# Layer 0 of a four-layer graph network: the first two output tiles take their products two weight tiles behind

## The chip, the cores and the metric

The kernel runs on one core of one Trainium2 chip. A time is the device time of one execution in microseconds. Four executions of the kernel before took 2601.92 to 2609.89 us, and their median is 2607.84 us.

## The reference, cut to what matters

Sixteen graphs of 1024 nodes with 256 features go through four layers. Each layer normalizes its input, applies a relu, runs a graph layer and adds the result to its input. The first of the four is the one that is changed:

```python
h = jnp.maximum(_layernorm(x, axis=-1), 0.0)
x = x + _L0_gnn_ref(h, adj, L0_gnn_W, L0_gnn_a)

def _L0_gnn_ref(input, adj, W, a):
    h = jnp.matmul(input, W)
    f1 = jnp.einsum('bnf,f->bn', h, a1)      # a1, a2: the two halves of a
    f2 = jnp.einsum('bnf,f->bn', h, a2)
    e = jax.nn.leaky_relu(f1[:, :, None] + f2[:, None, :], negative_slope=ALPHA)
    logits = jnp.where(adj > 0, e, NEG_BIG)
    attention = jax.nn.softmax(logits, axis=1)
    h_prime = jnp.matmul(attention, h)
    return jax.nn.elu(h_prime)
```

The softmax runs over the rows (axis 1), so each column of the attention has a sum of its own. Layer 1 is the same with a softmax along the other axis, layer 2 averages over the neighbours with the plain adjacency, and layer 3 has four heads with a normalization behind it.

## The kernel before, in words

Nodes are cut into eight tiles of 128. For layer 0 of one graph the kernel first projects the eight node tiles (`project`, line 690, evicted at line 770). The logit terms of all nodes are laid out as a row in DRAM and read back to all partitions (lines 709 and 715); the first graph makes this row on TensorE instead. Then comes the loop over j = 0 to 7 that the change touches. For each j it makes one weight tile `p` of 128x1024 on VectorE: line 800 takes the larger of two products, line 802 multiplies by the mask and sums, and line 803 takes the reciprocal of the sum. Line 804 on ScalarE scales row tile j of `hs` by it. Weight tile j then serves all eight output tiles i: output tile i is the sum over j of `p[j]` (columns of i) times `hs[j]`. That is `product(ps, i, j)`, line 790.

Two of the eight output tiles (four in the first graph) are called early. They have their PSUM banks from the start of the loop, and their products are issued inside it. The other output tiles follow after the loop, one after another, each with its eight products, in the two banks of the pool `at_ps`. So output tile 2 needs the bank that output tile 0 held, which comes free when ScalarE has read it at lines 822 and 824. After each pair of output tiles the residual is written and the next layer's norm of that pair begins (lines 759, 760, 639, 671, 684).

TensorE carries out one f32 product of 128x128 with 128x256 as two passes. The products of one weight tile for two output tiles are thus four passes, shown as x4 in the rows. Layer 2 uses a rounded form of f32 with one pass for each of its adjacency products (line 922, with `hi` and `lo` parts), and f32 for the product at line 916.

Graphs overlap. The work of graph b is written as a generator that yields an estimate of time after each step, and a queue (lines 1045 to 1097) interleaves the generators by these times. Graph b+1 starts 120 units after graph b. A scheduler behind the language then sets the order in each engine's queue from its own estimates, and each engine takes its queue strictly in that order. `later(...)` is `tc.keep_in_program_order`: such an instruction keeps its place among the others that are marked. In the steady state layer 0 of a graph runs beside layer 2 of the graph before it, so the early products stand in TensorE's queue between the adjacency products of line 922.

The places that the prediction's steps touch are these: the loop and `product` of `layer0` (lines 784 to 826), the eviction of layer 2's output tiles (lines 930 and 931 on ScalarE, 932 and 760 on VectorE), the norm of the next layer (`pair` at line 639, `shifted` at line 671, `flip` at lines 684 and 685), and layer 3's projection, line 690 again, with its eviction at line 945. The loads of the adjacency are issued on POOL's queue (line 589) when an output tile of layer 2 has freed its buffer.

Of the kernel before, what the change touches and what calls it, by code (L numbers as in the profile page):

```python
# [421 lines left out]
def tile_simple_stack(  # L422
# [13 lines left out]
    NT = N // P  # L436
# [250 lines left out]
    def project(norm, w, n, width):  # L687
        ps = mm_ps.tile([P, HALF], F32, tag="mm", name="ps_proj")
        for c in range(DC):
            nc.tensor.matmul(ps[:, :width], norm.ht[:, c, n * P : (n + 1) * P], w[:, c, :width], start=(c == 0), stop=(c == DC - 1))  # L690
        return ps

    def new_hs(name="hs"):
        return state.tile([P, NT, W3], F32, tag="hs", name=name, bufs=3)

    def spread(col, n, scales, name):

        k = n * NT
        ps = tr_ps.tile([P, P], F32, tag="tr", name="ps_col")
        nc.tensor.transpose(ps[:k, :], col, ident)
        all_rows = []
        for scale in scales:
            e = small.tile([H * NT, P], F32, tag="e_row", name="e_row", bufs=2)
            nc.scalar.activation(e[:k, :], ps[:k, :], AF.Exp, scale=scale)
            d = dram.tile([n, N], F32, tag=f"row_{name}", name="d_row", bufs=4)
            later(nc.sync.dma_start(d.rearrange("r (t p) -> (r t) p", p=P), e[:k, :]))
            all_rows += [d[r] for r in range(n)]  # L710
        return all_rows

    def everywhere(d, tag):
        row = work.tile([P, N], F32, tag=tag, name="row", bufs=2)
        later(nc.sync.dma_start(row, d.partition_broadcast(P)))
        return row
# [20 lines left out]
    def column(src, n):  # L737

        col = small.tile([P, H, NT], F32, tag="col", name="col", bufs=2)
        nc.vector.tensor_copy(col[:, :n, :], src.rearrange("p t n -> p n t"))  # L740
        return col[:, :n, :].rearrange("p n t -> p (n t)")

    def watch(b, layer, terms):
        k = b * 3 + layer
        nc.vector.tensor_reduce(top[:, k : k + 1], terms, axis=AX.XY, op=OP.max, apply_absolute_value=True)

    def weights(name):
        return work.tile([P, N], F32, tag="p", name=name, bufs=NT)

    def residual(xs, i, v, after, e=None):  # L750

        x = xs[:, i, :]
        if i % 2 == 0:
            if i == NT - 2:
                after.settle()
            after.flip()
            after.sums = small.tile([P, 2], F32, tag="sums", name="sums")
        if e is not None:
            nc.vector.scalar_tensor_tensor(x, e, 1.0, x, op0=OP.min, op1=OP.add)  # L759
        nc.vector.scalar_tensor_tensor(x, v, 0.0, x, op0=OP.max, op1=OP.add, accum_out=after.sums[:, i % 2 : i % 2 + 1])  # L760
        if i % 2:
            after.pair(xs, i // 2, after.sums)


    def layer0(b, xs, m, norm, after):
        hs = new_hs()
        by_pe = Row() if b == 0 else None
        for n in range(NT):
            ps = project(norm, wx[0], n, D + 2)
            nc.scalar.activation(hs[:, n, : D + 2], ps[:, : D + 2], AF.Copy, scale=norm.rs[n])  # L770
            if by_pe:
                by_pe.add(n, hs[:, n, D : D + 1])
            m.step()
            yield 0.98
        mask = m.bytes
        if by_pe:
            row_a, row_b = by_pe.rows((1.0, S))
        else:
            row_a, row_b = [everywhere(d, "row") for d in spread(column(hs[:, :, D : D + 1], 1), 1, (1.0, S), "l0")]
        q = small.tile([P, NT], F32, tag="q", name="q")  # L780
        nc.scalar.activation(q, hs[:, :, D + 1], AF.Exp, scale=1.0 - S)
        watch(b, 0, hs[:, :, D : D + 2])
        yield 5.42
        ps_ = []
        early = [at_ps.tile([P, HALF], F32, tag="at", name="ps_o0") for _ in range(EARLY)]
        if b == 0:
            early += [hd_ps.tile([P, HALF], F32, tag="hd", name="ps_o0") for _ in range(NHALF)]

        def product(ps, i, j):
            m = nc.tensor.matmul(  # L790
                ps[:, :D], ps_[j][:, i * P : (i + 1) * P], hs[:, j, :D], start=(j == 0), stop=(j == NT - 1)
            )
            if i < len(early) and j < 7:
                later(m)

        for j in range(NT):
            if m.raws:
                m.step(2)
            p = weights("p0")
            nc.vector.scalar_tensor_tensor(p, row_a, q[:, j : j + 1], row_b, op0=OP.mult, op1=OP.max)  # L800
            z = small.tile([P, 2], F32, tag="z", name="z", bufs=8)
            nc.vector.scalar_tensor_tensor(p, p, 1.0, mask[:, j, :], op0=OP.mult, op1=OP.mult, accum_out=z[:, 0:1])
            nc.vector.reciprocal(z[:, 1:2], z[:, 0:1])
            nc.scalar.activation(hs[:, j, :D], hs[:, j, :D], AF.Copy, scale=z[:, 1:2])  # L804
            ps_.append(p)
            if b == 0:
                gates.append(p)
            for i, ps in enumerate(early):
                if j:
                    product(ps, i, j - 1)  # L810
            yield 2.7
        for i, ps in enumerate(early):
            product(ps, i, NT - 1)
        for i in range(NT):
            if i < len(early):
                ps = early[i]
            else:
                ps = at_ps.tile([P, HALF], F32, tag="at", name="ps_o0")
                for j in range(NT):
                    product(ps, i, j)  # L820
            e = work.tile([P, D], F32, tag="e", name="e")
            nc.scalar.activation(e, ps[:, :D], AF.Exp)  # L822
            v = work.tile([P, D], F32, tag="v", name="v")
            nc.scalar.copy(v, ps[:, :D])  # L824
            residual(xs, i, v, after, e)
            yield 3.74
# [218 lines left out]
    def graph(b):  # L1045
        xs = loaded.pop(b)
        m = masks.pop(b)
        norm = Norm()
        for g in range(NT // 2):
            norm.pair(xs, g)  # L1050
            m.step()
            yield 2.55
        for layer, inputs in ((layer0, (m,)), (layer1, (m.bytes,)), (layer2, ())):
            yield 2.36
            norm.settle()
            norm.flip()
            after = Norm(degrees(b) if layer is layer1 else None)
            yield from layer(b, xs, *inputs, norm, after)
            norm = after
        yield 1.44  # L1060
        norm.flip()
        res = state.tile([P, NT, H, HW], F32, tag="res", name="res", bufs=1)
        hs = yield from layer3(b, xs, m.bytes, norm, res)
        return tail(b, xs, hs, res)
# [25 lines left out]
    while queue:  # L1090
        queue.sort(key=lambda g: g[:2])
        at, b, g = queue.pop(0)
# [21 lines left out]
    ps = tr_ps.tile([P, P], F32, tag="tr", name="ps_bad")  # L1114
# [64 lines left out]
```

## Time and profile before

| what | value |
|---|---|
| median of four executions | 2607.84 us (2601.92 to 2609.89) |
| the profiled execution's own time | 2611.11 us |
| span of that execution | 2609.2 us |
| granted TensorE clock, mean | 0.985 |
| TensorE matmul busy | 2463.9 us, 94% |
| VectorE busy | 1977.3 us, 76% |
| ScalarE busy | 1432.3 us, 55% |

Times in the rows count from the start of the span. A row of the timeline has its start, its length, the engine, the line in the kernel, the operation, the tiles written and read, the shapes, and the number of instructions that were merged into it. In square brackets stand the idle time of that engine before the row and what ended it. PE is the matmul side of TensorE and PEld its weight loads. A matmul's end is modelled, so the distance from one start to the next is what a pass costs. In the view of waits, a line has who waited for whom, the sum, the number of times and the longest.

### The profile page before, as it was taken

The page shows a single profiled execution, that of the slowest core. Times are in us where ns is not written, and L with a number is a line of the kernel's source. Part 1 is how long each engine was busy: PE and PEld are TensorE (multiplying, and loading weights), DVE is VectorE, ACT ScalarE, POOL GpSimd, SP SyncE. Part 2 cuts the span into 40 slices and gives each one's busy share as a digit, 9 for nine tenths or more (in the row PEclk, how much of TensorE's full clock was granted, in tenths as well). Part 3 has the DMA queues.
Part 4 walks back from the last instruction along what each step waited for, and adds up shares of the span by engine and source line. Part 5 has one row for each costly group of instructions (what it writes and reads, how often), then busy time and mean ns, then how long its engine had stood idle before and what let it go on. Part 6 is the DMA issues. An engine that isn't in the chain of part 4 may idle for free.

```text
span 2609.2 us, 63088 instructions
## 1 busy us (share of the span) xinstructions
PE 2463.9 (94%) x26224; PEld 2103.2 (81%) x26224; DVE 1977.3 (76%) x3862; ACT 1432.3 (55%) x4036; POOL 450.3 (17%) x454
## 2 busy tenths in 40 slices
PE   5999999999999999999999999999999999999975
PEld 4788888888878888888888878888887888878864
DVE  6458778687787877778697777878778687787858
ACT  3663755637565473755637465573755637565350
POOL 1010211203012130211203012120211203111021
PEclk8899999999999999999999999999999999999997
DMA  4541522615225261422615225161521615224031
GB/s 128 119 86 55 130 62 69 138 51 143 65 72 119 70 134 55 129 63 67 145 52 140 68 76 114 64 134 55 134 58 62 134 59 145 65 69 105 26 65 36
DMA packets 212153, 232.17 MB, mean 89 GB/s; under 512 B 10345, under 2 KB 160977, under 8 KB 211857
## 3 DMA queue, kind: packets, MB, share of 16 engines
q0 software_dynamic: 137728, 83.90, 17.4%
q1 hardware_dynamic: 74128, 144.14, 16.9%
q8 instruction: 208, 3.41, 0.5%
q14 instruction: 89, 0.72, 0.1%
HBM read 210.78 MB, written 17.22 MB: 87 GB/s over the span
## 4 chain that ended last, share of the span: by engine, by line
PE 57%; DVE 16%; DMA 10%; ACT 10%; issue 4%; POOL 2%; SPq 0%; DVEq 0%; POOLq 0%; ACTq 0%
PE ps_o L790 16%; PE ps_proj L690 12%; PE ps_o L981 9%; DVE p L968 7%; PE ps_o L922 6%; PE ps_o L854 6%; PE pt_h L684 5%; DMA raw<-in_adj_t 4%; DVE p L861 4%; DMA row<-d_row 4%; PE ps_o L916 3%; ACT mask L581 3%; ACT hn L671 2%; ACT unread L644 2%; DMA d_row<-e_row 1%
## 5 line engine op out<-in xcount | busy, mean ns | idle before, releaser
L968 DVE SCALAR_TENSOR_TENSOR p<-row,q,mask 128x1024 f32<-128x1024 f32 x512 | 631.8, 1278 | 64.9 <-PE ps_o L981 55.8
L981 PEld LDWEIGHTS ps_o<-hb,p 128*64 128x64 f32 x16384 | 505.8, 138 | 103.2 <-issue 41.3
L981 PE MATMUL ps_o<-hb,p 128*64 128x65 f32 x16384 | 542.0, 224 | 29.7 <-DVE p L968 18.2
L690 PE MATMUL ps_proj<-wx,ht 128*128 128x258 f32 (+2 forms) x2048 | 509.7, 388 | 3.6 <-ACT hs L770 2.3
L790 PE MATMUL ps_o<-hs,p 128*128 128x256 f32 x2048 | 492.4, 385 | 16.4 <-ACT hs L804 16.4
L854 PE MATMUL ps_o<-hs,p 128*128 128x257 f32 x2048 | 499.1, 390 | 6.2 <-DVE p L861 6.2
L790 PEld LDWEIGHTS ps_o<-hs,p 128*128 128x128 f32 x2048 | 379.4, 191 | 72.4 <-ACT hs L804 20.8
L690 PEld LDWEIGHTS ps_proj<-wx,ht 128*128 128x128 f32 x2048 | 366.0, 191 | 77.6 <-ACT hs L770 9.8
L854 PEld LDWEIGHTS ps_o<-hs,p 128*128 128x128 f32 x2048 | 376.1, 192 | 61.0 <-DVE p L861 8.0
L596 POOL TENSOR_SCALAR rs<-mv 128x4 f32<-128x4 f32 (+1 forms) x112 | 41.2, 368 | 1558.2 <-ACT unread L644 1536.5
L597 POOL TENSOR_TENSOR rs<-rs,neg_half 128x4 f32<-128x4 f32 (+2 forms) x144 | 261.8, 1818 | 11.8
L759 DVE SCALAR_TENSOR_TENSOR xs<-e,xs 128x256 f32<-128x256 f32 x256 | 107.7, 421 | 183.4 <-ACT e L822 136.2
L671 ACT ACTIVATE hn<-xs,shift 128x256 f32<-128x256 f32 x384 | 175.3, 502 | 123.5 <-DVE shift L639 116.2
L684 PE MATMUL pt_h<-ident,hn 128*128 128x128 f32 x1024 | 181.0, 288 | 39.6 <-ACT hn L671 38.6
L922 PE MATMUL ps_o<-hi,adj 128*128 128x258 f32 x1024 | 202.8, 321 | 1.7
L684 PEld LDWEIGHTS pt_h<-ident,hn 128*128 128x128 f32 x1024 | 115.3, 142 | 106.4 <-ACT hn L671 89.9
L589 POOL DMA_DIRECT2D adj<-in_adj x128 | 114.7, 896 | 477.6 <-PE ps_o L922 475.9
L581 ACT ACTIVATE mask<-raw 128x512 uint8<-128x512 int32 x240 | 150.1, 626 | 65.4 <-DMA raw<-in_adj_t 38.4
L760 DVE SCALAR_TENSOR_TENSOR xs<-v,xs 128x256 f32<-128x256 f32 x384 | 160.6, 421 | 29.4 <-ACT v L824 16.5
L989 ACT ACTIVATE res<-ps_o 128x260 f32<-128x260 f32 x128 | 46.4, 375 | 232.7 <-PE ps_o L981 232.4
L800 DVE SCALAR_TENSOR_TENSOR p<-row,q 128x1024 f32<-128x1024 f32 x128 | 161.3, 1270 | 15.3 <-DMA row<-d_row 13.7
L922 PEld LDWEIGHTS ps_o<-hi,adj 128*128 128x128 f32 x1024 | 152.2, 190 | 14.3 <-ACT hi L908 5.0
(115 smaller groups left out, 3035.0 us busy)
## 6 DMA issues: line engine op xcount, KB each, us to landing
raw<-in_adj_t SPq DMA_DIRECT2D x256, 256.0 KB
adj<-in_adj POOLq DMA_DIRECT2D x128, 512.0 KB, 4.7
row<-d_row SPq DMA_DIRECT2D x109, 512.0 KB
xs<-in_x POOLq DMA_DIRECT2D x32, 512.0 KB, 6.9
out<-xs SPq DMA_DIRECT2D x32, 512.0 KB
wx<-in_w SPq DMA_DIRECT2D x3, 256.0 KB
d_row<-e_row SPq DMA_DIRECT2D x45, 4.0 KB
wts<-in_w_t SPq DMA_DIRECT2D x2, 256.0 KB
```

The source lines that it names most:

```text
L581: nc.scalar.activation(to, raw, AF.Square, accum_out=total)
L597: nc.gpsimd.tensor_tensor(rs[:, :n], rs[:, :n], neg_half[:, :n], op=OP.pow)
L671: nc.scalar.activation(hn, xs[:, 2 * g + k, :], AF.Relu, scale=scale, bias=bias)
L684: nc.tensor.transpose(pt[:, c, k * P : (k + 1) * P], hn[:, c * P : (c + 1) * P], ident)
L690: nc.tensor.matmul(ps[:, :width], norm.ht[:, c, n * P : (n + 1) * P], w[:, c, :width], start=(c == 0), stop=(c == DC - 1))
L760: nc.vector.scalar_tensor_tensor(x, v, 0.0, x, op0=OP.max, op1=OP.add, accum_out=after.sums[:, i % 2 : i % 2 + 1])
L790: m = nc.tensor.matmul(ps[:, :D], ps_[j][:, i * P : (i + 1) * P], hs[:, j, :D], start=(j == 0), stop=(j == NT - 1))
L800: nc.vector.scalar_tensor_tensor(p, row_a, q[:, j : j + 1], row_b, op0=OP.mult, op1=OP.max)
L854: nc.tensor.matmul(ps[:, : D + 1], ps_[j][:, i * P : (i + 1) * P], hs[:, j, : D + 1], start=(j == 0), stop=(j == NT - 1))
L922: nc.tensor.matmul(ps[:, : D + 2], adj_n[j][:, i, :], h[:, i, : D + 2], start=False, stop=(h is lo and i == NT - 1), skip_group_check=True,)
L968: nc.vector.scalar_tensor_tensor(p, row, q[:, jj, h : h + 1], mask[:, jj, :], op0=OP.max, op1=OP.mult)
L981: nc.tensor.matmul(pss[g][part, k * HW : (k + 1) * HW], ps_[t][:, i * P : (i + 1) * P][:, part], hbv[:, j + t, h, :], start=(j == 0 and t ...
```

## The change

In all graphs but the first, the early products of weight tile j - 2 are issued in step j of the loop, where before they were those of weight tile j - 1. Two weight tiles are therefore left over after the loop instead of one. Those two are issued tile by tile, each for both output tiles. The mark that keeps the early products in program order ends one tile sooner in these graphs, at j below 6 in place of j below 7. The first graph has the same order as before. No instruction is added or removed.

```diff
             m = nc.tensor.matmul(
                 ps[:, :D], ps_[j][:, i * P : (i + 1) * P], hs[:, j, :D], start=(j == 0), stop=(j == NT - 1)
             )
-            if i < len(early) and j < 7:
+            if i < len(early) and j < NT - behind_by:
                 later(m)
 
+        behind_by = 1 if b == 0 else 2
         for j in range(NT):
...
             for i, ps in enumerate(early):
-                if j:
-                    product(ps, i, j - 1)
+                if j >= behind_by:
+                    product(ps, i, j - behind_by)
             yield 2.7
-        for i, ps in enumerate(early):
-            product(ps, i, NT - 1)
+        for j in range(NT - behind_by, NT):
+            for i, ps in enumerate(early):
+                product(ps, i, j)
```

## The prediction, made before the result was known

> **What bounds the kernel now.** I read the page first, for the busy engines and the chain that ended last:
>
> ```profile
> PE 2463.9 (94%) x26224; PEld 2103.2 (81%) x26224; DVE 1977.3 (76%) x3862; ACT 1432.3 (55%) x4036; POOL 450.3 (17%) x454
> ...
> PE 57%; DVE 16%; DMA 10%; ACT 10%; issue 4%; POOL 2%; SPq 0%; DVEq 0%; POOLq 0%; ACTq 0%
> ...
> L790 PE MATMUL ps_o<-hs,p 128*128 128x256 f32 x2048 | 492.4, 385 | 16.4 <-ACT hs L804 16.4
> ```
>
> TensorE (PE) is the bound. In the whole run its products of line 790 wait 16.4 us for the scaled rows of line 804: the most that a longer lag could cover. Next the view of waits, for the first 60 us (the first graph, which the change leaves alone) and for a window around layer 0 of graph 3:
>
> ```profile
> PE ps_o L790 <- ACT hs L804: 8.1, 3, 6.6
> ```
>
> ```profile
> PE ps_o L790 <- ACT hs L804: 1.3, 1, 1.3
> ```
>
> So 8.1 of the 16.4 us are out of reach, and 8.3 are left for fifteen graphs. In each of graphs 2 to 15 it is one wait, of 0.2 to 1.7 us. The timeline of TensorE for graph 3 shows where it stands and how full TensorE is behind it:
>
> ```profile
> 475.27 1.13 PE L790 MATMUL ps_o<-hs,p 128*128 128x256 f32 x4 [1.30 <-ACT hs L804]
> ...
> 479.26 1.03 PE L916 MATMUL ps_o<-wx,ht 128*128 128x256 f32 x4
> 480.12 1.89 PE L790 MATMUL ps_o<-hs,p 128*128 128x256 f32 x8
> ...
> 484.75 1.03 PE L790 MATMUL ps_o<-hs,p 128*128 128x256 f32 x4
> ...
> 486.64 1.13 PE L790 MATMUL ps_o<-hs,p 128*128 128x256 f32 x4
> ...
> 494.09 1.03 PE L790 MATMUL ps_o<-hs,p 128*128 128x256 f32 x4
> ...
> 495.68 1.08 PE L790 MATMUL ps_o<-hs,p 128*128 128x256 f32 x4
> ...
> 498.26 3.62 PE L790 MATMUL ps_o<-hs,p 128*128 128x256 f32 x16
> 501.71 1.05 PE L690 MATMUL ps_proj<-wx,ht 128*128 128x264 f32 x4
> ```
>
> The one wait is that of tile 0's products (475.27). The tiles after it find their rows ready: 480.12 holds tiles 1 and 2, then tiles 3, 4, 6 and 7 (5 is left out). The chain of waits runs over TensorE alone from 475.27 to 549.19, so a delay put in here is paid in full unless a later wait swallows it. Last, ScalarE's rows in the same window, then all engines' just behind it:
>
> ```profile
> 488.83 0.91 ACT L671 ACTIVATE hn<-xs,shift 128x256 f32<-128x256 f32 x2 [2.24 <-DVE shift L639]
> ...
> 493.18 0.51 ACT L804 ACTIVATE hs<-hs,z 128x256 f32<-128x256 f32 x1 [1.17 <-DVE z L803]
> ...
> 496.77 0.36 ACT L822 ACTIVATE e<-ps_o 128x256 f32<-128x256 f32 x1
> ```
>
> ```profile
> 500.56 0.29 DVE L639 TENSOR_SCALAR shift<-sums 128x2 f32<-128x2 f32 x2
> ...
> 502.61 0.64 PEld L684 LDWEIGHTS pt_h<-ident,hn 128*128 128x128 f32 x6 [0.26 <-ACT hn L671]
> ...
> 503.77 0.20 PEld L684 LDWEIGHTS pt_h<-ident,hn 128*128 128x128 f32 x2 [0.25 <-ACT hn L671]
> ...
> 506.35 2.52 PEld L690 LDWEIGHTS ps_proj<-wx,ht 128*128 128x128 f32 x12 [0.37 <-ACT hs L945]
> ```
>
> Here TensorE meets ScalarE just in time, three times. What makes ScalarE later here is paid.
>
> **The change, part by part.** In the built program the queues of POOL and SP are unchanged; the change issues no DMA. No instruction is added, so at the row's pace (16 passes in 501.71 - 498.26 = 3.45 us, 0.216 each) the work is the same.
>
> *Tile 0.* Its products keep their place in TensorE's queue in all fifteen graphs, between the same two products of line 922. The wait of 0.2 to 1.7 us stays. Gain 0.
>
> *Graphs 2 to 15, TensorE's order.* Tile 2 moves behind the next layer-2 output tile (call these by number: 4 follows tile 1) and joins tile 3; tile 4 joins tile 5; tiles 6 and 7 stand later, among the `lo` products of output tiles 6 and 7. The transposes of line 684 move too, and come to stand between `hi` products twice. Weight loads that show: a group of line 790 entered from line 922 takes 1.13 us (486.64), from line 916 1.03 (484.75), so 0.10. Before, tiles 4 and 5 pay it, tile 7 half (1.08); three transpose pairs behind line 922 pay about 0.05 each (rows of 0.43 and 0.44 against 0.38). Together 0.40. After, tiles 6 and 7 pay 0.10 each and four transpose pairs 0.05: 0.40 again. Net 0.
>
> By the Trainium skill, "TensorE: Matmul & The Clock Gate", section "Step-by-step: what each phase is for", the queue pulls the next weight load ahead of running matmuls, so no change of form should cost anything. The 0.10 rows speak against that for loads behind line 922. The rule makes both sums 0 and the rows make both 0.40, so the difference is the same by either.
>
> *ScalarE's and VectorE's order.* ScalarE takes line 930 of output tile 5 ahead of the line 671 pair at 488.83. That tile now ends near 488.02 on TensorE (before 488.93; nothing of line 790 is inside it), so lines 930 and 931 are through by 488.6. Queued behind them are that pair, lines 644 and 804; free by 0.2 us. VectorE takes the reciprocal of tile 6 ahead of tile 7's line 800, so line 804 at 493.18 starts near 492.3. Tile 6 is ready for its place at 492.87.
>
> *The walk.* From 479.26, the same in both, I set TensorE's queue in its new order with the starts of the rows (four passes of line 790 0.86, eight of line 922 1.15 or 0.97, line 916 as 0.43 for two passes) and let each step wait for ScalarE's row:
> - tiles 2 and 3 at 483.78;
> - the transposes of the pair 488.83 could start at 489.21 but the pair's halves are ready at 489.33 and 489.79: 0.12 and 0.07 lost;
> - tiles 4 and 5 at 490.06, tile 6 at 492.87, tile 7 at 497.04 (before 495.68), its rows ready at 496.95;
> - output tile 2 (498.26 before) at 498.80, but with two passes of layer 3's projection (0.44) already done: 0.10 late. Its bank is read out by 498.55, so no wait;
> - lines 822 and 824 of output tile 0 wait for tile 7: line 822 goes from 496.77 to 497.85, also behind line 685. VectorE has both residuals still to do behind that, and line 639 comes at 501.21 instead of 500.56: 0.65 late;
> - so line 671 and the transposes at 502.61 come at 503.25 where TensorE could be at 503.13; output tile 3 starts at 504.69 against 504.49: 0.20 late;
> - the third projection waits for line 945, now 0.65 late: 507.00 against 506.35, with two more passes (0.43) of output tile 3 done: 0.22 late. From there the order is that of before.
>
> All graphs 2 to 15 start this walk with a wait at tile 0, so engines stand alike in them: 14 x 0.22 = 3.1 us.
>
> *POOL.* Line 589 is issued when a layer-2 output tile ends: tiles 4 and 5 about 1.4 and 0.9 us sooner, 6 about 0.9 later. They load for the next graph, 4.7 us to land and 150 us ahead of use. The norm's lines 596 and 597 behind them wait for ScalarE as before. Cost 0; if the cover went, 0.9 once a graph.
>
> *Graph 1.* Only TensorE's order differs: tile 3 and two transpose pairs leave line 922 and two pairs go there, about -0.1 us.
>
> Sum: +3.0 us. The profiled execution took 2611.11 us, of which 2609.2 is its span; it would take 2614.1. It stands 0.13% above the median, 2607.84, so I take 2610.8 for the median. Bounds of the walk: if all three gaps ahead of the weight loads above (0.26, 0.25, 0.37) went, each graph would gain 0.88, or 12.3 us; if the 0.65 reached TensorE in full on top of 0.12 and 0.07, each would lose 0.84, or 11.8 us. The rows are nearer the middle, where TensorE still has work while ScalarE is late.
>
> **The rivals.** A measurement of this kernel can't tell less than about 0.2%, 5.2 us, from no change.
> - *Slower, by a bank wait.* Output tile 2 has its bank 0.25 us before it is due. If lines 822 and 824 come more than 0.25 us later than walked, TensorE stands still at 498.8, and line 639 is later still. At 0.5 us later: 0.25 there plus the same at line 945, about 0.7 a graph, +10 us: 2618. For it: ScalarE takes lines 644 and 685 first. Against: its rows from 488 to 499 have idle spans of 1 to 2 us.
> - *Faster.* VectorE frees tile 6's rows 0.9 us sooner and output tile 5 ends 0.9 us sooner. If that brings line 639 at 500.56 forward instead of back, the three gaps shrink; by half, 0.44 a graph, -6 us: 2602. It decides if line 639 comes before 500.3. Against: line 639 hangs on output tile 0's read-out, which hangs on tile 7, 1.4 us later.
> - *Swallowed.* The 0.22 goes into the next wait on the row read back from DRAM (row ready, then tile 0): 2607.8. Against: that row is itself made from TensorE's work, so it shifts along.
>
> **How the numbers follow.** The walk 0.40, swallowed 0.10: both within 0.2%. The bank wait and other ways in which ScalarE is later 0.32, the faster case 0.18. I predict 2610.8 us; the walk's own range is 2605 to 2614. Leaving out the outer half of the two outer cases gives 2600 to 2619. Within 0.2% 0.50, slower 0.32, faster 0.18.
>
> **What would show it.** The wait of tile 0 unchanged at 0.2 to 1.7 us in graphs 2 to 15. Line 790 of tiles 2 and 3 as one row of x8, and tiles 4 and 5 as another. From the first products of a graph to the x16 row 23.5 us instead of 22.99; from there to line 690's x12 row 8.2 instead of 8.09. Line 639 of the two pairs 0.65 us later against tile 0's start. Wrong would be: tile 0's wait gone, a gap ahead of the x16 row, or a graph's period that moves by over 0.4 us.

## The result, and the profile after

The changed kernel takes 2612.72 us (median of 47 executions, 2606.05 to 2622.68), the kernel before 2607.33 us on the same chips (73 executions). The ratio is 1.0024, with a 95% interval of 1.0018 to 1.0030: 6.3 us slower, 4.7 to 7.8 (the two medians alone differ by 5.4). The profiled execution of after has a span of 2611.1 us at a mean granted clock of 0.986 (before 2609.2 at 0.985). A single execution thus shows only 1.9 us of it, and the reading has to go by the distances inside a graph.

The page after, first its busy engines, then the chain that ended last, then the group of line 790:

```profile
PE 2465.9 (94%) x26224; PEld 2103.6 (81%) x26224; DVE 1975.9 (76%) x3862; ACT 1437.6 (55%) x4036; POOL 434.3 (17%) x454
...
PE 51%; DVE 24%; DMA 10%; ACT 10%; issue 3%; POOL 2%; SPq 0%; DVEq 0%; POOLq 0%; ACTq 0%
...
L790 PE MATMUL ps_o<-hs,p 128*128 128x256 f32 x2048 | 487.1, 384 | 14.5 <-ACT hs L805 14.5
```

The page gives almost nothing away. The same engine is busy for the same share, and line 790 even waits 1.9 us less than before. (The change adds one line at 796 and another at 813. So lines 800 to 804 of before are 801 to 805 here, and lines from 814 on have two more.) The view of waits has, beside line 790's, one line that moved by much. The transposes of line 684 waited 37 times for ScalarE's line 671 before, 38.6 us in all. Now it is 52 times:

```profile
PE pt_h L684 <- ACT hn L671: 42.8, 52, 3.8
...
PE ps_o L790 <- ACT hs L805: 14.5, 17, 6.6
```

TensorE's timeline of one graph, the tenth counted from zero, shows the new wait in its place:

```profile
1571.32 1.13 PE L790 MATMUL ps_o<-hs,p 128*128 128x256 f32 x4 [0.34 <-ACT hs L805]
...
1579.89 1.89 PE L790 MATMUL ps_o<-hs,p 128*128 128x256 f32 x8
...
1585.88 0.44 PE L684 MATMUL pt_h<-ident,hn 128*128 128x128 f32 x2 [0.40 <-ACT hn L671]
...
1586.56 1.89 PE L790 MATMUL ps_o<-hs,p 128*128 128x256 f32 x8
...
1589.37 1.03 PE L790 MATMUL ps_o<-hs,p 128*128 128x256 f32 x4
...
1595.03 3.62 PE L790 MATMUL ps_o<-hs,p 128*128 128x256 f32 x16
...
1603.24 2.94 PE L690 MATMUL ps_proj<-wx,ht 128*128 128x264 f32 x12
```

Tile 0's products still wait (0.34 us here). Tiles 2 and 3 stand together, as do tiles 4 and 5. Ahead of tiles 4 and 5 the transposes wait 0.40 us by the bracket. A bracket counts from the modelled end of the passes before it; counted from the starts it is 0.55 us, where my walk had 0.12. (The four passes of line 924 ahead of them take 0.67 us in before when nothing waits, 0.31 for the first and 0.12 for each of the others. Here the transposes start 1.22 us behind the first.) To see why, take all engines around that spot, first before (its tile 0 started at 1570.75), then after (1571.32). Only the rows of lines 589, 639, 671 and 684, and after also of line 934, are shown:

```profile
1584.12 0.16 DVE L639 TENSOR_SCALAR shift<-sums 128x2 f32<-128x2 f32 x1
...
1584.32 0.91 ACT L671 ACTIVATE hn<-xs,shift 128x256 f32<-128x256 f32 x2 [2.24 <-DVE shift L639]
...
1584.88 0.88 POOL L589 DMA_DIRECT2D adj<-in_adj  x1 [3.75 <-PE ps_o L922]
1584.88 0.44 PE L684 MATMUL pt_h<-ident,hn 128*128 128x128 f32 x2
```

```profile
1584.44 0.88 POOL L589 DMA_DIRECT2D adj<-in_adj  x1 [4.15 <-PE ps_o L924]
...
1584.69 0.59 DVE L639 TENSOR_SCALAR shift<-sums 128x2 f32<-128x2 f32 x1
1584.77 0.52 DVE L934 TENSOR_TENSOR v<-v,row_bias 128x256 f32<-128x256 f32 x1
...
1585.32 0.91 ACT L671 ACTIVATE hn<-xs,shift 128x256 f32<-128x256 f32 x2 [0.62 <-DVE z L804]
1585.88 0.20 PEld L684 LDWEIGHTS pt_h<-ident,hn 128*128 128x128 f32 x2 [0.60 <-ACT hn L671]
1585.88 0.44 PE L684 MATMUL pt_h<-ident,hn 128*128 128x128 f32 x2 [0.40 <-ACT hn L671]
```

Against tile 0's start line 639 comes at 13.37 us in both. What moved is POOL: its issue of line 589 stood at 14.13 us, behind line 639, and now stands at 13.12, ahead of it. And line 639, two values per partition, takes 0.59 us in place of 0.16 and ends with the issue. Line 671, the transposes and all behind them wait for it. (The bracket of line 671 names line 804, the last semaphore by the profile. But line 671 reads `shift`, which line 639 makes, and line 639 ends at 1585.28, with line 804.)

Line 639 is held like this 13 times in the profile of after, once in each of graphs 2 to 15 but graph 5, and never in that of before. The medians over graphs 2 to 15, in us from tile 0's start (empty where before has the tiles apart):

| event | before | walk (prediction) | after |
|---|---|---|---|
| tiles 2 and 3 | | 8.51 | 8.57 |
| tiles 4 and 5 | | 14.79 | 15.23 |
| tile 6 | 18.82 | 17.60 | 18.04 |
| tile 7 | 20.40 | 21.77 | 22.04 |
| row x16 (output tile 2) | 22.98 | 23.53 | 23.70 |
| line 639 of the last pairs | 25.30 | 25.94 | 26.13 |
| output tile 3 | 29.22 | 29.42 | 29.61 |
| layer 3's column (line 703) | 41.00 | 41.22 | 41.41 |

The last row is the figure that I use from here on, since the same work is done by then in both kernels. A graph loses 0.41 us. In the two graphs where the held line 639 is one pair later, it loses 0.64. Graph 5 has no held row. VectorE stands some 0.5 us closer behind tile 0 there (its line 639 comes at 12.88 us), and the figure is 40.72. Before has one graph like that too (graph 4, with 12.78 and 40.45), so I take the 0.2 of the walk for graph 5, which is an estimate. Then eleven graphs by 0.41, two by 0.64 and one by 0.2 give 6.0 us; measured were 6.3.

### The profile page after: what moved, and what is told of

Its sections match the earlier page's. It is cut to its first block, busy times and chain, and to the rows that moved or that the text cites. A ratio compares the mean times of both kernels' runs of the same rounds, so it can differ in the third digit from the quotient of the medians.

```text
span 2611.1 us, 63104 instructions
## 1 busy us (share of the span) xinstructions
PE 2465.9 (94%) x26224; PEld 2103.6 (81%) x26224; DVE 1975.9 (76%) x3862; ACT 1437.6 (55%) x4036; POOL 434.3 (17%) x454
## 4 chain that ended last, share of the span: by engine, by line
PE 51%; DVE 24%; DMA 10%; ACT 10%; issue 3%; POOL 2%; SPq 0%; DVEq 0%; POOLq 0%; ACTq 0%
PE ps_o L790 13%; PE ps_proj L690 12%; PE ps_o L983 11%; DVE p L970 7%; PE ps_o L856 6%; PE pt_h L684 4%; DVE p L801 4%; DMA row<-d_row 4%; DVE p L863 4%; DVE p L803 4%; DMA raw<-in_adj_t 4%; PE ps_o L924 3%; ACT mask L581 2%; ACT hn L671 2%; ACT unread L644 2%
## 5 line engine op out<-in xcount | busy, mean ns | idle before, releaser
L790 PE MATMUL ps_o<-hs,p 128*128 128x256 f32 x2048 | 487.1, 384 | 14.5 <-ACT hs L805 14.5
L597 POOL TENSOR_TENSOR rs<-rs,neg_half 128x4 f32<-128x4 f32 (+2 forms) x144 | 250.5, 1740 | 11.8
```

The lines of the kernel that those rows point to most:

```text
L597: nc.gpsimd.tensor_tensor(rs[:, :n], rs[:, :n], neg_half[:, :n], op=OP.pow)
L790: m = nc.tensor.matmul(ps[:, :D], ps_[j][:, i * P : (i + 1) * P], hs[:, j, :D], start=(j == 0), stop=(j == NT - 1))
```

## The experiments

*Theory A:* two costs add up. One is the walk of the prediction: output tile 0 is read out later, because tile 7's products come later. The other is that output tile 5 of layer 2 ends sooner, POOL issues line 589 sooner, and this issue holds VectorE's line 639. *Theory B:* the second cost is ScalarE's new order (output tile 5's eviction ahead of the line 671 pair), and the long row is only a sign of it. *Theory C:* there is no second cost, the late read-out is just larger than I walked.

**Line 639 in another form, in after.** The work is the same, but VectorE multiplies by a constant tensor instead of a scalar. The order is that of after in the whole of the stretch that I measure. (Some 60 us behind tile 0, VectorE and ScalarE have two neighbours swapped in each graph, and the next run has the same swaps.)

```diff
+    per_d = const.tile([P, 2], F32, name="per_d")
+    nc.vector.memset(per_d, -1.0 / 256)
...
-                nc.vector.tensor_scalar(shift, sums, -1.0 / D, None, op0=OP.mult)
+                nc.vector.tensor_tensor(shift, sums, per_d, op=OP.mult)
```

> The kernel after, with the 128x2 line 639 as a product of two tensors (tensor_tensor with a constant of -1/256) in place of tensor_scalar; the queues are those of after but for this form. Theory A (a VectorE line 639 that starts inside POOL's DMA issue of line 589 is held to its end, 0.59 us in place of 0.17, once in each of graphs 2 to 15): tensor_tensor isn't held. All rows of line 639 stay under 0.25 us, the wait of the transposes behind it falls from 0.40 us to about 0.12, and from the first products to layer 3's column a graph takes about 41.2 us in place of 41.41 (before: 41.00). Against before about +3 us, 1.001. Theory B (ScalarE's new order, line 932 of output tile 5 ahead of the pair of line 671, makes the pair late): nothing changes, 0.40 and 41.41 stay, +6 us, 1.0024. Theory C (only the late read-out of output tile 0 behind tiles 6 and 7 counts): as B, +6 us.

The same spot of graph 10 in that kernel (its lines are two higher; tile 0 at 1573.05):

```profile
1586.15 0.88 POOL L591 DMA_DIRECT2D adj<-in_adj  x1 [4.10 <-PE ps_o L926]
...
1586.42 0.15 DVE L641 TENSOR_TENSOR shift<-sums,per_d 128x2 f32<-128x2 f32 x1
...
1586.61 0.91 ACT L673 ACTIVATE hn<-xs,shift 128x256 f32<-128x256 f32 x2 [0.20 <-DVE shift L641]
...
1587.17 0.20 PEld L686 LDWEIGHTS pt_h<-ident,hn 128*128 128x128 f32 x2 [0.19 <-ACT hn L673]
1587.18 0.44 PE L686 MATMUL pt_h<-ident,hn 128*128 128x128 f32 x2
```

POOL's issue starts 0.27 us ahead of line 641, as in after, but the row takes 0.15 us. The transposes start 14.13 us behind tile 0, in after 14.56. Their PE row has no bracket, but a gap under 0.15 us gets none: counted from the starts as above, 0.14 us is left (0.81 less 0.67), near the 0.12 of the walk. No row of the kernel is held. A graph takes 41.19 us, against 41.41 in after and 41.00 in before. So the held row costs 0.22 us a graph, and 0.19 remain that are not due to it. ScalarE's order has not changed, so B is out. C had 41.41 and is out too. The time agrees without deciding: 1.0018 (1.0006 to 1.0030), 4.7 us, where 14 x 0.19 = 2.7 lies within the interval, and so does after's 6.3. It is the trace that tells the two apart.

**The same form in before.**

> The kernel before with the same other form of line 639. It is there to see what the form alone does. Theory A: before has no held row of line 639, so 41.0 us a graph and 0 us, within 2 us either way. Theories B and C: the same. If the new form were itself faster or slower on the path, it shows here and is taken off the other run.

0.9996 (0.9981 to 1.0010), and 41.00 us a graph. The form has no value of its own, because before has nothing to hold.

**The front half of the change alone.** The early products of step j are given as a list in the graphs but the first. Tile 2 lags, tiles 2 and 3 come together, and the rest, with the mark that keeps the program's order, is as before. (In the built program tile 1 does not lag, here or in after: it comes 4.85 us behind tile 0, as in before.)

```diff
-            for i, ps in enumerate(early):
-                if j >= behind_by:
-                    product(ps, i, j - behind_by)
+            for jj in [j - 1] * (j > 0) if b == 0 else [[], [0], [1], [], [2, 3], [4], [5], [6]][j]:
+                for i, ps in enumerate(early):
+                    product(ps, i, jj)
             yield 2.7
...
-        for j in range(NT - behind_by, NT):
+        for j in [NT - 1] if b == 0 else [7]:
```

> Only the front half of the change: tiles 1 and 2 are left behind as in after, and the lag is caught up when tiles 2 and 3 are issued together; tiles 4 to 7 stand where before has them, and so do ScalarE's and VectorE's queues. Theory A: output tile 5 of layer 2 ends when it did before, so POOL's issue doesn't meet line 639: no row of 0.59 us, 41.0 us a graph, 0 us. Theories B and C: both put the cost behind tile 4, so also 41.0 us and 0 us. A theory that the cost is the lag at the front (tile 2 moved) has +0.2 to +0.4 us a graph, +3 to +6 us.

0.9999 (0.9987 to 1.0012), 41.02 us a graph, no held row. Moving tile 2 by one layer-2 output tile costs nothing. The issue of line 589 that follows output tile 4 does come 1.4 us sooner (8.11 in place of 9.51), but meets no line 639.

**The rear half alone.** The same edit with another list:

```diff
+            for jj in [j - 1] * (j > 0) if b == 0 else [[], [0], [1], [2], [], [3], [4, 5], [6]][j]:
```

> Only the rear half: tiles 0 to 3 stand where before has them, tiles 4 to 7 where after has them, and ScalarE's and VectorE's queues are those of after. Theory A: output tile 5 ends sooner again and POOL's issue meets line 639: one row of about 0.59 us in each of graphs 2 to 15, 41.3 to 41.5 us a graph, +5 to +7 us (1.0019 to 1.0027). Theory B: the same time, without need of the 0.59 rows. Theory C: the same. If the front half carries the cost: 41.0 to 41.2 us, 0 to +3 us.

1.0038 (1.0024 to 1.0052), about 10 us. That is more than the whole change, and more than I expected. The rows tell why. Here the issue comes 0.19 to 0.20 us ahead of line 639 of the first of the two pairs, which is not held, and 0.31 to 0.33 us ahead of that of the next pair, which is held. Graph 10, tile 0 at 1581.06:

```profile
1600.36 0.95 POOL L589 DMA_DIRECT2D adj<-in_adj  x1 [1.46 <-PE ps_o L924]
...
1600.68 0.61 DVE L639 TENSOR_SCALAR shift<-sums 128x2 f32<-128x2 f32 x1
...
1601.32 0.91 ACT L671 ACTIVATE hn<-xs,shift 128x256 f32<-128x256 f32 x2 [2.69 <-DVE z L804]
...
1601.88 0.44 PE L684 MATMUL pt_h<-ident,hn 128*128 128x128 f32 x2 [0.24 <-ACT hn L671]
```

In 13 of graphs 2 to 15 it is that pair, and a graph takes 41.65 us. Held at this place, the row costs 0.46 us more than with nothing held. All of its 0.43 us reaches line 639 of the last pairs, at 26.37 us against 25.93; in after, where the row is held one pair sooner, 0.20 does (26.13). That less of the graph is left here to make it up is my reading. In after the first pair is the one held in 11 graphs. There everything behind comes 0.2 to 0.3 us later, and the next issue and the next line 639 fall together, so that neither holds the other. In its two graphs of 41.64 us the first issue came 0.22 us ahead of line 639 and the second held it.

**The rear half with the other form of line 639.**

> The rear half alone with line 639 as a product of two tensors. The rear half alone took 41.65 us from a graph's first products to layer 3's column (before 41.00), with one row of line 639 of 0.59 to 0.61 us per graph. Theory A: without the held row what stays is the later read-out behind tiles 6 and 7, as in the whole change with that form: 41.15 to 41.25 us, and the product row x16 at 23.4 in place of 23.88. Theory B (the order of ScalarE): 41.65 stays. Against before about +3 us by A, +9 us by B.

41.19 us a graph, the row x16 at 23.44 us, no held row, as A has it. POOL's issue stands 0.31 to 0.33 us ahead of the row there too. The time is 1.0016 (0.9999 to 1.0033). Both kernels without held rows end on 41.19, and so the 0.19 us belongs to the rear half, where the walk had put it.

**Three weight tiles behind.**

```diff
-        behind_by = 1 if b == 0 else 2
+        behind_by = 1 if b == 0 else 3
```

> Three weight tiles behind in all graphs but the first. Tile 0's products keep their place in TensorE's queue once more, so its wait stays at 0.2 to 2 us a graph by every theory. Theory A: the cost does not grow with the lag; it is decided by where output tiles 4 to 6 of layer 2 end and whether an issue of line 589 then meets line 639. 0.2 us a graph with no row of 0.59 us, 0.4 to 0.65 with one, 1.0 or more with two: +3, +6 to +9, or +14 us. A theory that the lag itself costs has 0.41 for one tile more, so 0.8 us for two tiles more, +12 us, whatever line 639 does.

1.0037 (1.0022 to 1.0051), 9.6 us. A graph takes 41.64 us with one held row, in the same place as in the rear half alone. One more tile of lag thus adds 0.23 us a graph, not another 0.41, and that is what the second place of the held row costs more than the first (0.46 against 0.22). Tile 0 waits as before (0.2 to 1.8 us).

**Tile 1 before tile 0.** This and the next two runs ask whether tile 0's wait, which the change leaves alone, could be taken away at all. The lists are put into the kernel before; the sums are added in another order:

```diff
-                ps[:, :D], ps_[j][:, i * P : (i + 1) * P], hs[:, j, :D], start=(j == 0), stop=(j == NT - 1)
+                ps[:, :D], ps_[j][:, i * P : (i + 1) * P], hs[:, j, :D], start=(j == (0 if b == 0 or i >= EARLY else 1)), stop=(j == NT - 1)
...
+            for jj in [j - 1] * (j > 0) if b == 0 else [[], [], [1, 0], [2], [3], [4], [5], [6]][j]:
```

> The kernel before, but in all graphs but the first the early products take weight tile 1 before weight tile 0, and both are issued in step 2; the sums are added in another order. Tile 0's products, which waited 0.2 to 1.7 us in each of graphs 2 to 15 (8.3 us in all), now stand behind 23 more products of layer 2 and next to those of tile 1. VectorE's and ScalarE's queues are those of before. If TensorE's path is all that counts: the wait is gone, -0.3 to -0.6 us a graph, -5 to -8 us, 0.997 to 0.998. By theory A output tiles 2 and 3 of layer 2 end 0.9 us sooner, so two issues of line 589 come sooner; if one of them meets line 639, a row of 0.59 us takes about 0.4 us of it back, -1 to +1 us. If the time is set by the row read back from DRAM, TensorE waits elsewhere for as long: 0.

0.9999 (0.9985 to 1.0013): nothing, a miss for the gain that I expected, and not by a held row, of which there is none. ScalarE's scaled rows of tiles 0 and 1 in graph 10, and TensorE's first products:

```profile
1570.66 0.51 ACT L805 ACTIVATE hs<-hs,z 128x256 f32<-128x256 f32 x1 [0.60 <-DVE z L804]
...
1575.41 0.91 ACT L805 ACTIVATE hs<-hs,z 128x256 f32<-128x256 f32 x2 [3.63 <-DVE z L804]
```

```profile
1575.97 2.86 PE L790 MATMUL ps_o<-hs,p 128*128 128x256 f32 x12 [0.27 <-ACT hs L805]
```

The wait moved to tile 1, whose rows come 4.75 us behind those of tile 0, and is as long there (7.5 us over the graphs, before 8.3). In before the rows of tile 1 were through just ahead of its products, too (in graph 10 at 1575.4 and 1575.6). So the wait belongs to the pace of the rows, not to the place of one tile.

**The same with the other form of line 639.**

> The same with line 639 as a product of two tensors, so that no issue on POOL can hold it. Theory A: -5 to -8 us, 0.997 to 0.998, whether or not the run without it meets a held row. If the time is set by the row read back from DRAM: 0.

0.9994 (0.9979 to 1.0009). The same again.

**Four behind.** The first early products come in step 4, tiles 1, 0, 2 and 3 together, again with tile 1 as the start of the sums:

```diff
+            for jj in [j - 1] * (j > 0) if b == 0 else [[], [], [], [], [1, 0, 2, 3], [4], [5], [6]][j]:
```

> As in the run with tile 1 first, but nothing early is issued until step 4, where tiles 1, 0, 2 and 3 come together; after that one tile behind as in the kernel before. In TensorE's queue tiles 0 to 4 now stand in one block behind two transpose pairs, some 9 us behind the old place of tile 0, when VectorE and ScalarE have long made the rows of tiles 0 and 1. With tile 1 first the wait had only moved to tile 1, whose rows come 4.7 us behind those of tile 0. If these waits are what a graph loses (7 to 8 us in graphs 2 to 15), they are gone and the time falls by 5 to 8 us, 0.997 to 0.998. If the row read back from DRAM and VectorE's pace behind it set the end, another wait of the same size takes their place (at the transposes behind line 671, or at tile 4): 0 within 2 us. By theory A a row of line 639 of 0.59 us may come in as well, since output tiles 2 to 4 of layer 2 end sooner: up to +0.65 us a graph, +9 us.

1.0057 (1.0037 to 1.0077), 15 us slower. That is worse than any of the expectations. The waits on rows are gone in graphs 1 to 15. A new one has come, in the view of waits and in graph 10:

```profile
PE ps_o L918 <- ACT edges L933: 22.3, 14, 2.9
```

```profile
1586.49 1.13 PE L918 MATMUL ps_o<-wx,ht 128*128 128x256 f32 x4 [1.36 <-ACT edges L933]
```

```profile
1583.93 0.91 ACT L805 ACTIVATE hs<-hs,z 128x256 f32<-128x256 f32 x2 [3.81 <-DVE z L804]
1585.91 0.47 ACT L932 ACTIVATE v<-ps_o,z 128x256 f32<-128x256 f32 x1 [1.07 <-DVE xs L760]
1586.29 0.15 ACT L933 COPY edges<-ps_o 128x1 f32<-128x1 f32 x1
```

Without early products between them, TensorE runs through layer 2's output tiles so fast that output tile 5 wants its PSUM bank before ScalarE has read output tile 3 out of it. ScalarE's queue has the scaling of tiles 1 and 2 ahead of that reading, which waits 3.81 us for VectorE, and then another 1.07 us for line 760. The 22.3 us of this are more than the 7 to 8 us that were saved. So the early products of tiles 0 to 2 also give ScalarE and VectorE the time to empty the banks.

**The same with the other form of line 639.**

> The same with line 639 as a product of two tensors: no held row by theory A. -5 to -8 us if the waits on rows are what is lost, 0 if another wait takes their place. The difference to the run without that form is what held rows cost it.

1.0028 (1.0012 to 1.0044), with the same bank wait (1.38 us in the graph of the same place, 21.9 in all). Neither kernel has a held row in its profile, so theory A doesn't explain why this one is some 7 us ahead of the other. The intervals overlap a little. The granted clock differs as well: on average it was 0.984 in the eight executions of the first and 0.986 in the twelve of the second, and among the executions of either kernel 0.001 of clock goes with some 2 us. By this estimate the clock makes about 4 of the 7 us, and the rest stays open. None of the runs beats the kernel before.

## Why the prediction was right or wrong

- *What bounds the kernel, tile 0, and the queue's order:* right. Tile 0's products still wait 0.17 to 1.70 us in graphs 2 to 15. The gain of 0 holds, and the runs with tile 1 first and four behind show that the wait is hard to get at: it moves to tile 1, or a bank wait takes its place. One size was off: I took 0.10 us for a group of line 790 behind line 922 from the lengths of rows, whose ends are modelled. By the starts in before, its first pass takes 0.285 us there and 0.216 behind line 916, so 0.07. Both sums shrink alike, and the net of 0 stays.
- *The walk:* right, nearly to the row, for the kernel in which nothing is held. The kernel after with the other form of line 639 has 8.56 us for tiles 2 and 3, 14.80 for 4 and 5, 17.62, 21.76, 23.44 for the row x16, 25.93 for line 639, 29.40 for output tile 3, and (graph 10) 31.70 for the x12 row, where the walk had 31.73. The net loss of 0.22 us a graph measured 0.19.
- *The step that failed is POOL's: "Cost 0; if the cover went, 0.9 once a graph."* I saw that line 589 would be issued 0.9 us sooner and asked only when its data would land. I did not ask what runs beside the issue itself. It came to stand on line 639, held it for 0.43 us, and made the transposes late: 0.22 us a graph where it hits the first pair, 0.46 where it hits the next. So the term put at 0 measured about 3.3 us (eleven graphs by 0.22 and two by 0.45), while the walk's term of 3.1 us (14 x 0.22) measured 2.7 (14 x 0.19). In the walk the same place shows as "0.12 and 0.07 lost"; the first of the two was 0.55 in after and 0.14 without the held row, counted from the starts.
- *Graph 1:* about -0.1 us was predicted; 40.94 before and 40.93 after.
- *The rivals:* "slower, by a bank wait" had the sign, but not the cause: after has no gap ahead of the x16 row. That mechanism is real in this kernel, though, as four behind shows at another bank. "Faster" fell because line 639 of the last pairs came later, as walked. "Swallowed" fell too, by the executions: 6.3 us is no less than the 6.0 that the graphs lose. The two profiled spans, 1.9 us apart, can't show it.
- *The numbers:* 2612.72 us is within the range and 1.9 above the forecast. That says little for the mechanism, since the range of 2600 to 2619 would have held no change as well as a loss of nearly twice the size: about half of the loss came from a cause that I had put at nothing. The likeliest case, within 0.2%, was missed by a little: 0.24% slower. Of the signs that I named for being wrong, the last came closest: the distance inside a graph moved by 0.41 us. The period of the graphs itself varies by several us in each profile (154.9 to 159.5 in before) and can't show so little.

## What to carry to other kernels

When an edit makes one engine's step end sooner, follow what that end triggers, and lay the triggered instruction itself over the others' queues: a DMA issue on POOL is 0.9 us of work beside VectorE and may not be free for it. Compare the same small instruction's duration before and after (here one row of 0.16 against 0.59 us), since totals of 2600 us hide it. And a wait that looks like a misplaced instruction may be the pace of its producer: with tile 0's products moved some 5 us back, it was still there.

## What was not expected of the hardware

The groups of line 639 over the whole run, in before, after, and after with the other form (busy us, mean ns, idle time before):

```profile
L639 DVE TENSOR_SCALAR shift<-sums 128x2 f32<-128x2 f32 x128 | 20.3, 164 | 1.2
```

```profile
L639 DVE TENSOR_SCALAR shift<-sums 128x2 f32<-128x2 f32 x128 | 26.0, 209 | 1.2
```

```profile
L641 DVE TENSOR_TENSOR shift<-sums,per_d 128x2 f32<-128x2 f32 x128 | 19.4, 156 | 0.7
```

The 5.7 us between the first two are thirteen rows of 0.58 to 0.61 us. Over the runs with the form of before, a line 639 that starts up to 0.23 us into a POOL issue of 0.81 to 0.95 us takes its usual 0.16 to 0.17 us (24 rows). One that starts 0.25 to 0.33 us into it ends 30 ns ahead of the issue's end, after 0.58 to 0.61 us (39 rows). Three that start 0.60 us into it end there too, after 0.24 us. So a row that starts later than some point between 0.23 and 0.25 us into the issue is held to its end, and one that has started before runs through. The tensor form, at the offsets of the held rows, is not held (40 rows in after and in the rear half alone with that form).

The Trainium skill, "SBUF — State Buffer", section "Who interferes with whom", names a port pair of SBUF that VectorE and GpSimd (the engine of the POOL rows) share. `tensor_scalar` can take it in a two-port mode, and the one that comes second "fully blocks". `tensor_tensor` has no such mode; with both inputs in SBUF it uses the pair's read side alone. The rows of 0.59 against 0.15 us fit that. That it is this port pair is the page's account, and no run here shows it; nor do the rows show the hold from the first moment of the issue.
